# Counting the guard flag in pieces and reordering the last images of a ViT tower kernel

## The chip, the cores and the metric

The kernel runs on one core of one Trainium2 chip. The metric is the device time of one execution in microseconds (us); lower is better. The number of a kernel is the median of several runs.

## The reference

The reference is a small vision transformer tower on 32 images of 3x256x256 in float32. Every image gives 256 tokens of 256 features.

```python
h = tokenizer(x)                                   # 16x16 patches, a matmul
h = h + L0_attn(layernorm(h))                      # gated attention with squared relu
h = h + L0_ffn(layernorm(h))                       # top half of the tokens through an MLP
h = h + L1_attn(layernorm(h))                      # phase memory
h = h + L1_ffn(layernorm(h))                       # this change lies here
```

Only the last line matters for this change. The layer-1 FFN makes four heads of 64 features, gives each head four experts that are causal softmax attentions, mixes them by a gate, adds a residual, normalizes, runs two small layers with a norm, and weights the heads by a last gate:

```python
sx = einsum(x, hl_w) + hl_b                        # heads
qkv = softmax(causal(q k)) v                       # four experts of each head
qkv = where(sx == 0, 0, qkv)                       # pad
mixed = sum over experts of out * softmax(gate)
resid = sx[arange(nh), arange(nh)]                 # head n of image n: four images feed every image
hn = layernorm(mixed + resid)
hx = relu(where(fx == 0, 0, fx @ fc1.T + b1)); hx = where(fx == 0, 0, hx @ fc2.T + b2)
fout = layernorm(hx + fx)
out = fout * softmax(fout @ fgate_w.T)
```

The two `== 0` masks and the ranges of some intermediate values are not applied in the fast path. The kernel counts zeros and values out of range, and if any was found it runs a slow general version afterwards.

## The kernel before

The tower is one function, `vit_tower`, with the stages one after the other. The layer-1 FFN is the last stage. It works image by image. The work of an image is cut into 93 pieces (`PIECES`, numbered from 0), each a small function of the image `b`: `heads` (3), `heads_out` (4), `experts` (5 and 7), `scores` (12 to 17), `exponentials` (18 to 23), `later_keys` (24 to 29), `outputs` (31 to 38), the gates, `scaled` (65), `turn_e` (66), the two small layers (69 to 73), `head_gate` (78 to 86) and `last_norm` (87 to 91).

The order of all instructions is written out by hand. `tc.manual_schedule` keeps every engine in the order in which the program issues. `ROUND` is a list of pairs (back, piece): in round `r` the piece is issued for image `r - back`, so several images are in flight at different depths. When the heads of the last image (piece 3 of image 31) have been issued, `END` takes over: a list of (images from the end, piece) for the rest, so (0, k) is image 31, (1, k) is image 30, and so on.

What each engine does in this stage: TensorE (PE) runs the heads, scores, outputs and layers into eight PSUM banks (`bank()`); ScalarE (ACT) copies and exponentiates them; GpSimd (POOL) masks the later keys (`later_keys`, L1237); VectorE (DVE) does gates, norms and sums; SyncE (SP) issues the transfers, in order. Each engine works through its own queue in order.

Names that the change and the prediction touch:

- `residual` (piece 1, L1145 to L1151) multiplies four heads of images 0 to 3 by the identity into a bank ("bank<-ident,sx") and copies them to `res` on DVE; for image 3 it then runs `centred`, three DVE instructions (L667 to L669). It reads `im.sx`, which `heads_out` of the same image has just written on ACT (L1162).
- `res` is read by `summed` (piece 61, L1332) of every image.
- `count_zeros` (L1170) runs one DVE pass over a 128x512 tile and leaves a count in a column of `zeros` (64 columns: `sx` and `fxT` of each image).
- `check_ranges` (L1263) compares the `ranges` of eight images (128x384) with two limits and multiplies the results into `good`. It runs for images 7, 15 and 23 inside the stage and for 31 behind it.
- Behind the hand-written order come the sums (L1571 to L1583): `n_bad` is the number of bad ranges and zeros of each partition, a matmul with `ones` sums it over the partitions, and DVE copies the sum to `flag` as an integer.
- `again = nc.values_load(flag[0:1, 0:1])` (L1586) loads the flag on all five engines, and `tc.If(again > 0)` (L1587) jumps over `general`, the slow version, which has several hundred instructions.
- `last_norm` (L1458) makes the output of an image in the tile `fout`. That tile has one buffer, so the next image's first write waits until the output transfer of the image before it (`out_dram<-fout`, L1473) has read it.
- `eblk` is a tile of the same shape, into which `turn_e` writes for all images but the last. Image 31 is turned on PE instead.

Of the kernel before, what the change touches and what calls it, by code (L numbers as in the profile page):

```python
# [33 lines left out]
F32 = mybir.dt.float32  # L34
# [6 lines left out]
P = 128  # L41
# [39 lines left out]
def vit_tower(tc, a, out):  # L81
# [1027 lines left out]
    with (  # L1109
# [10 lines left out]
        def whole(im, name, shape, pool=None, key=None):  # L1120

            key = key or name
            if key not in im.whole:
                im.whole[key] = (pool or p1).tile(shape, F32, name=name)
            return im.whole[key]
# [42 lines left out]
                nc.sync.dma_start(im.sw[halves[1 - h], :, :], im.sx[halves[h], :, :])  # L1168

        def count_zeros(x, k):  # L1170
            junk = p1.tile([P, 2 * N], F32, name="junk")
            nc.vector.tensor_scalar(  # L1172
                junk, x.rearrange("p h n -> p (h n)"), 0.0, 0.0, ALU.is_equal, ALU.add, accum_out=zeros[:, k : k + 1]
            )
# [84 lines left out]
        def in_range(b, first, n):  # L1259
            return ranges[:, b // 8 % 2, b % 8, first : first + n]  # L1260

        def check_ranges(b):
            r = ranges[:, b // 8 % 2, :, :].rearrange("p b x -> p (b x)")  # L1263
            nc.vector.scalar_tensor_tensor(good, r, 1.0 / LOW, good, ALU.is_le, ALU.mult)
            nc.vector.scalar_tensor_tensor(good, r, 1.0 / HIGH, good, ALU.is_ge, ALU.mult)

        def small(name, shape):
            return spool.tile(shape, F32, name=name, tag=f"{name}_{shape[1]}", bufs=4)
# [187 lines left out]
                nc.vector.tensor_tensor(im.gate, im.gate, over(im.m, [P, NC, NH], 2), ALU.mult)  # L1456

        def last_norm(b, im, i):  # L1458
            f = whole(im, "fout", G8)
            if i == 0:  # L1460
                nc.vector.tensor_tensor(f, im.whole["ey"][:, :, 0:HD], over(im.rs, G8, 2), ALU.mult)  # L1461
            if i == 1:
                nc.vector.tensor_tensor(f, f, over(row_e("fn_g"), G8, 1), ALU.mult)
            if i == 2:
                nc.vector.tensor_tensor(f, f, over(row_e("fn_b"), G8, 1), ALU.add)  # L1465
            if i in (3, 4):
                for n in range(NH):
                    g, d = (i - 3) * NH + n, slice(n * HD, (n + 1) * HD)
                    nc.vector.scalar_tensor_tensor(  # L1469
                        f[:, g, :], f[:, g, :], im.gate[:, i - 3, n : n + 1], H[b][:, i - 3, d], ALU.mult, ALU.add  # L1470
                    )
            if i == 5:
                nc.sync.dma_start(  # L1473
                    out[b].rearrange("(c p) d -> p c d", p=P),
                    f.rearrange("p (c n) d -> p c (n d)", n=NH),
                )
# [17 lines left out]
            (squares_sum, 1), (root, 1), (head_gate, 0), (head_gate, 1), (head_gate, 2), (head_gate, 3),  # L1494
            (head_gate, 4), (head_gate, 5), (head_gate, 6), (head_gate, 7), (head_gate, 8), (last_norm, 4),
            (last_norm, 0), (last_norm, 1), (last_norm, 2), (last_norm, 3), (last_norm, 5),
            (features_moved,),
        )
        ROUND = (
            (-1, 84), (-4, 43), (-5, 27), (-4, 46), (-6, 5), (-5, 13), (-4, 44), (-6, 6), (-1, 85), (-1, 86),  # L1500
            (-1, 90), (-5, 19), (-5, 25), (-5, 12), (-5, 28), (-2, 2), (-2, 67), (-4, 47), (-4, 48),
            (-5, 14), (-5, 18), (-5, 24), (-1, 91), (-3, 60), (-4, 49), (-3, 61), (-5, 30), (-6, 7), (-6, 9),
            (-2, 69), (-4, 50), (-3, 62), (-7, 3), (-2, 92), (-5, 20), (-2, 68), (-4, 51), (-4, 52),
            (-3, 63), (-5, 26), (-5, 17), (-2, 70), (-6, 8), (-3, 64), (-7, 4), (-7, 1), (-6, 10), (-4, 53),
            (-6, 16), (-6, 11), (-6, 15), (-4, 54), (-2, 71), (-4, 55), (-5, 23), (-6, 22), (-5, 29),
            (-5, 34), (-4, 56), (-4, 57), (-5, 32), (-3, 65), (-5, 37), (-4, 58), (-3, 66), (-2, 72),
            (-2, 73), (-6, 21), (-2, 74), (-5, 42), (-4, 59), (-2, 75), (-2, 76), (-5, 45), (-9, 0),
            (-5, 33), (-2, 77), (-5, 31), (-2, 87), (-2, 78), (-2, 79), (-2, 89), (-5, 41), (-5, 39),
            (-5, 40), (-5, 38), (-2, 80), (-5, 35), (-2, 81), (-2, 88), (-2, 82), (-5, 36), (-2, 83),
        )  # L1510
        END = (
            (5, 68), (3, 51), (0, 2), (3, 52), (3, 53), (3, 55), (3, 54), (2, 20), (2, 17), (3, 56), (5, 92),
            (1, 10), (1, 11), (4, 63), (5, 70), (3, 57), (1, 8), (1, 16), (1, 15), (4, 64), (4, 65), (0, 4),
            (2, 26), (3, 58), (2, 23), (5, 71), (4, 66), (3, 59), (5, 73), (5, 72), (3, 60), (2, 29),
            (1, 21), (2, 32), (1, 22), (2, 31), (5, 74), (5, 75), (1, 30), (4, 2), (2, 36), (5, 76), (2, 37),
            (2, 45), (2, 38), (3, 61), (5, 77), (3, 62), (2, 39), (5, 87), (2, 34), (3, 63), (2, 40),
            (2, 33), (5, 78), (5, 89), (5, 79), (2, 46), (2, 35), (1, 14), (2, 44), (3, 64), (2, 43),
            (2, 42), (1, 13), (2, 41), (5, 88), (3, 65), (4, 67), (0, 5), (2, 47), (5, 80), (2, 48), (2, 49),
            (5, 81), (2, 50), (1, 20), (5, 82), (2, 51), (2, 52), (3, 66), (1, 19), (4, 92), (4, 69), (0, 6),
            (2, 53), (5, 83), (1, 12), (0, 7), (4, 70), (5, 84), (1, 27), (2, 54), (0, 9), (5, 85), (2, 55),  # L1520
            (2, 56), (1, 17), (2, 57), (5, 90), (5, 86), (1, 28), (1, 26), (0, 10), (2, 58), (1, 18),
            (1, 24), (0, 11), (0, 8), (2, 59), (0, 15), (1, 23), (1, 25), (0, 16), (4, 71), (3, 2), (4, 72),
            (1, 29), (1, 31), (0, 21), (0, 22), (5, 91), (4, 73), (4, 68), (2, 60), (1, 36), (0, 27),
            (1, 34), (1, 33), (4, 74), (3, 67), (4, 75), (1, 32), (1, 44), (2, 61), (4, 76), (2, 62),
            (1, 38), (1, 41), (1, 39), (4, 77), (4, 87), (1, 42), (4, 78), (4, 79), (2, 63), (1, 40),
            (4, 80), (4, 89), (2, 64), (1, 37), (2, 65), (1, 35), (2, 66), (4, 81), (1, 46), (1, 45),
            (0, 13), (0, 28), (1, 43), (4, 82), (1, 47), (1, 48), (0, 14), (0, 19), (1, 49), (4, 88),
            (3, 69), (0, 20), (1, 50), (4, 83), (0, 25), (3, 92), (1, 51), (1, 52), (3, 70), (0, 12),
            (1, 53), (3, 68), (0, 18), (4, 84), (0, 26), (4, 85), (1, 54), (2, 2), (1, 55), (0, 17), (4, 86),
            (0, 34), (0, 35), (0, 24), (0, 43), (1, 56), (0, 23), (0, 33), (0, 31), (0, 29), (1, 57),  # L1530
            (4, 90), (3, 71), (0, 39), (0, 41), (0, 42), (0, 32), (2, 67), (0, 36), (1, 58), (3, 72),
            (3, 73), (3, 74), (0, 38), (4, 91), (2, 92), (1, 59), (0, 44), (3, 75), (0, 40), (3, 76),
            (0, 37), (0, 46), (2, 69), (0, 45), (1, 60), (3, 77), (1, 61), (3, 78), (0, 47), (3, 79),
            (0, 48), (1, 62), (2, 70), (1, 63), (0, 49), (1, 64), (3, 87), (3, 80), (2, 71), (1, 65),
            (3, 81), (0, 50), (1, 66), (3, 82), (3, 83), (3, 89), (3, 84), (0, 51), (0, 52), (3, 88),
            (0, 53), (3, 85), (2, 68), (1, 2), (0, 54), (0, 55), (3, 86), (2, 72), (0, 56), (3, 90), (2, 73),
            (2, 74), (0, 57), (2, 75), (2, 76), (0, 58), (3, 91), (2, 77), (1, 67), (1, 69), (1, 92),
            (0, 59), (2, 78), (2, 87), (2, 79), (0, 60), (2, 80), (2, 89), (1, 70), (2, 81), (1, 71),
            (2, 82), (0, 61), (2, 83), (2, 88), (2, 84), (0, 62), (2, 85), (0, 63), (0, 64), (2, 90),
            (2, 86), (0, 65), (1, 72), (1, 73), (1, 74), (1, 68), (0, 66), (0, 67), (1, 75), (2, 91),  # L1540
            (0, 69), (0, 92), (1, 76), (1, 77), (0, 70), (1, 87), (0, 71), (1, 78), (1, 79), (1, 89),
            (1, 80), (1, 81), (1, 82), (1, 88), (1, 83), (1, 84), (0, 72), (1, 85), (0, 73), (1, 90),
            (1, 86), (0, 74), (0, 75), (0, 76), (0, 30), (0, 77), (1, 91), (0, 78), (0, 79), (0, 80),
            (0, 81), (0, 87), (0, 82), (0, 83), (0, 89), (0, 84), (0, 88), (0, 85), (0, 90), (0, 86),
            (0, 91), (0, 1), (0, 68),
        )
        LAST = PIECES.index((heads,))

# [10 lines left out]
        with tc.manual_schedule(engines={ENG.PE, ENG.DVE, ENG.Activation, ENG.Pool, ENG.SP}):  # L1559
# [3 lines left out]
            for b, k in order_e():  # L1563
                do, *i = PIECES[k]
                do(b, images[b], *i)
                if do == heads_out and b in LATE:
                    last_features(LATE[b])
        check_ranges(B - 1)


        n_bad = p1.tile([P, 2], F32, name="n_bad")  # L1571
        nc.vector.tensor_reduce(n_bad[:, 0:1], good, AX.X, ALU.add)
        nc.vector.tensor_reduce(n_bad[:, 1:2], zeros, AX.X, ALU.add)
        nc.vector.scalar_tensor_tensor(
            n_bad[:, 0:1], n_bad[:, 0:1], -1.0, n_bad[:, 1:2], ALU.mult, ALU.add
        )
        nc.vector.tensor_scalar(n_bad[:, 0:1], n_bad[:, 0:1], float(8 * N_RANGE), None, ALU.add)
        ones = p1.tile([P, 1], F32, name="ones")
        nc.vector.memset(ones, 1.0)
        p = bank()  # L1580
        mm(p[0:1, 0:1], n_bad[:, 0:1], ones)
        flag = cpool.tile([1, 1], mybir.dt.int32, name="flag")
        nc.vector.tensor_copy(flag, p[0:1, 0:1])  # L1583

    right_e.close()
    again = nc.values_load(flag[0:1, 0:1])  # L1586
# [385 lines left out]
```

## Time and profile before

| what | us |
|---|---|
| time, median of 3 runs | 1864.86 (1863.34 to 1864.94) |
| the profiled execution, its own time | 1866.7 |
| its span, from the first to the last instruction | 1864.9 |
| PE busy | 1815.6 (97%) |
| DVE busy | 1349.6 (72%) |
| ACT busy | 811.0 (43%) |
| POOL busy | 615.6 (33%) |
| mean granted TensorE clock | 0.987 of full speed |

Busy is the time in which an engine had an instruction in execution. The span is cut into 40 slices on the profile's page, each about 46.6 us, with the busy share of each engine in tenths. The layer-1 FFN begins at about 1243 us, in slice 27; the last image's heads (where `END` begins) run at 1778 us; the last arithmetic instruction starts at 1858.99 us.

### The profile page before, as it was taken

What the parts mean: (1) busy time and instruction counts of PE and PEld (TensorE: products, weight loads), DVE (VectorE), ACT (ScalarE), POOL (GpSimd) and SP (SyncE); (2) the same over time, 40 slices, a digit from 0 to 9 for tenths busy, and PEclk for the clock granted to TensorE, in tenths of its full rate; (3) what the DMA queues carried; (4) which work ended last, traced back from release to release, by engine and by line L of the source; (5) the groups of instructions that cost most, each with busy time, mean ns of one, the idle gap of its engine ahead of it and who ended that gap; (6) DMA issues with size and microseconds to landing.
All of it is one profiled execution on the core that took longest, in us unless ns stands there. A gap on an engine that the chain in (4) does not pass through costs nothing.

```text
span 1864.9 us, 36574 instructions
## 1 busy us (share of the span) xinstructions
PE 1815.6 (97%) x14282; PEld 1274.4 (68%) x14282; DVE 1349.6 (72%) x3592; ACT 811.0 (43%) x1640; POOL 615.6 (33%) x696
## 2 busy tenths in 40 slices
PE   9999999999999999999999999999999999999993
PEld 7887567676766677666654555567777887878871
DVE  2335377878787664543578887754899999999998
ACT  0001222222222211211345545547888888888882
POOL 1223143434343334332444334332223222232230
PEclk9999999999999999999999999999999999999995
DMA  9540222221212135333222222222344443443332
GB/s 302 159 152 27 46 45 58 54 60 48 55 45 58 43 106 152 96 116 93 88 77 80 79 79 80 79 68 54 95 106 107 105 108 101 105 108 103 102 94 59
DMA packets 193171, 167.50 MB, mean 90 GB/s; under 512 B 70880, under 2 KB 166112, under 8 KB 192608
## 3 DMA queue, kind: packets, MB, share of 16 engines
q1 hardware_dynamic: 186272, 147.51, 27.8%
q0 software_dynamic: 6144, 16.79, 3.0%
q8 instruction: 115, 1.88, 0.4%
q10 hardware_dynamic: 576, 0.79, 0.1%
q14 instruction: 64, 0.52, 0.1%
HBM read 82.98 MB, written 57.41 MB: 75 GB/s over the span
## 4 chain that ended last, share of the span: by engine, by line
PE 91%; DVE 6%; ACT 1%; DMA 1%; issue 1%; SPq 0%; ACTq 0%; DVEq 0%
PE bank L118 90%; DVE fout L1469 1%; DVE eo L1318 0%; DMA patch<-in_patches_dram 0%; PE bank L516 0%; DVE two L1326 0%; DVE ranges L1341 0%; DVE six L126 0%; DVE junk L1172 0%; DVE ey L1426 0%; ACT dex L945 0%; DVE dz L991 0%; DVE fout L1465 0%; DVE fout L1461 0%; DVE dxB L199 0%
## 5 line engine op out<-in xcount | busy, mean ns | idle before, releaser
L1237 POOL TENSOR_SCALAR_AFFINE_SELECT et<-et 128x512 f32<-128x512 f32 (+1 forms) x192 | 169.3, 891 | 397.0 <-ACT et L1228 282.2
L1228 ACT ACTIVATE et<-bank 128x512 f32<-128x512 f32 x384 | 203.1, 625 | 0.4 <-PE bank L118 0.3
L118 PE MATMUL bank<-ev,et 128*64 128x68 f32 (+1 forms) x6144 | 193.4, 224 | 0.8 <-POOL et L1237 0.6
L118 PEld LDWEIGHTS bank<-ev,et 128*64 128x64 f32 x6144 | 189.8, 137 | 3.8 <-issue 1.2
L118 PE MATMUL bank<-g,sw 64*128 64x256 f32 (+1 forms) x512 | 180.3, 490 | 0.0
L118 PE MATMUL bank<-g,sx 64*128 64x256 f32 (+1 forms) x512 | 179.3, 490 | 0.3 <-ACT g L1190 0.3
L118 PE MATMUL bank<-tokW,patch 128*128 128x256 f32 x768 | 166.8, 380 | 2.9 <-DMA patch<-in_patches_dram 2.9
L118 PEld LDWEIGHTS bank<-tokW,patch 128*128 128x128 f32 x768 | 146.1, 191 | 24.0 <-issue 3.8
L118 PE MATMUL bank<-bxT,w_wuv 128*128 128x512 f32 x300 | 134.5, 604 | 2.7 <-DMA bxT<-b_turned 2.7
L118 PEld LDWEIGHTS bank<-g,sx 64*128 64x128 f32 x512 | 92.2, 187 | 54.3 <-issue 45.0
L864 ACT ACTIVATE hT<-bank,cols 128x512 f32<-128x512 f32 x64 | 44.0, 687 | 186.9 <-PE bank L118 186.9
L118 PE MATMUL bank<-wvo,dm 128*128 128x512 f32 x256 | 114.3, 599 | 0.0
L118 PE MATMUL bank<-w_wo,gT 128*128 128x256 f32 x512 | 113.2, 379 | 0.0
L118 PE MATMUL bank<-attn,bv 128*128 128x256 f32 x512 | 113.1, 379 | 0.0
L118 PE MATMUL bank<-w_w,hT 128*128 128x256 f32 x512 | 112.3, 379 | 0.0
L118 PE MATMUL bank<-xsel,w_w 128*128 128x512 f32 x256 | 111.4, 592 | 0.0
L118 PEld LDWEIGHTS bank<-attn,bv 128*128 128x128 f32 x512 | 97.2, 190 | 19.6 <-issue 7.2
L126 DVE BATCH_NORM_STATS2 six<-h 128x6 f32<-128x256 f32 x256 | 105.5, 412 | 4.4
L118 PEld LDWEIGHTS bank<-w_w,hT 128*128 128x128 f32 x512 | 97.0, 190 | 15.6 <-issue 2.9
L118 PEld LDWEIGHTS bank<-w_wo,gT 128*128 128x128 f32 x512 | 97.2, 190 | 13.4 <-DVE gT L489 0.2
L118 PEld LDWEIGHTS bank<-bxT,w_wuv 128*128 128x128 f32 x300 | 58.0, 194 | 69.9 <-issue 68.9
L118 PE MATMUL bank<-w_wuv,bxT 128*128 128x512 f32 x240 | 105.4, 592 | 0.0
(286 smaller groups left out, 3570.3 us busy)
## 6 DMA issues: line engine op xcount, KB each, us to landing
patch<-in_patches_dram SPq DMA_DIRECT2D x31, 768.0 KB, 4.6
exT<-normed SPq DMA_DIRECT2D x32, 256.0 KB, 3.7
sw<-sx SPq DMA_DIRECT2D x64, 128.0 KB, 2.4
out_dram<-fout SPq DMA_DIRECT2D x32, 256.0 KB, 2.1
er_turned<-eblk SPq DMA_DIRECT2D x31, 256.0 KB, 2.7
fraw<-er_turned SPq DMA_DIRECT2D x62, 128.0 KB, 3.2
both<-fxT SPq DMA_DIRECT2D x62, 128.0 KB, 2.3
both<-hx SPq DMA_DIRECT2D x62, 128.0 KB, 2.3
```

The costliest lines, as they stand in the source:

```text
L118: nc.tensor.matmul(o, lhsT, rhs, start=first, stop=last)
L126: nc.vector.bn_stats(six, x)
L864: nc.scalar.activation(s.hT[:, m, :], p, AF.Gelu_apprx_tanh, bias=col("b1", m))
L1228: nc.scalar.activation(t2[:, i, :], p, AF.Exp)
L1237: nc.gpsimd.affine_select(out=own, in_=own, pattern=[[0, 2 * n_e], [1, P]], compare_op=ALU.is_ge, fill=0.0, base=0, channel_multiplier=-1,)
L1469: nc.vector.scalar_tensor_tensor(f[:, g, :], f[:, g, :], im.gate[:, i - 3, n : n + 1], H[b][:, i - 3, d], ALU.mult, ALU.add)
```

## The change

Four things, all in the layer-1 FFN.

1. **The flag.** Four new pieces (`count_bad`, 93 to 96) do the counting of image 31 inside the hand-written order: the ranges of images 24 to 30 first (336 wide), then the zeros, then the ranges of image 31 alone (48 wide), then the sum over the partitions and the copy to `flag`. In `END` all four stand ahead of the last image's `last_norm`. Two products instead of one add up in the bank.
2. **An output tile of its own.** `last_norm` of image 31 writes into `eblk` instead of `fout`.
3. **The residual's product later.** In `ROUND`, (-7, 1) became (-6, 1): the product of image b is issued one round later and no longer behind `heads_out` of the same image.
4. **A new `END`.** The list is ordered anew as a whole; it holds the same pieces and the four new ones. The `ones` column is set on POOL instead of DVE.

```diff
         def count_zeros(x, k):
+            done.add(k)
...
-        def check_ranges(b):
-            r = ranges[:, b // 8 % 2, :, :].rearrange("p b x -> p (b x)")
-            nc.vector.scalar_tensor_tensor(good, r, 1.0 / LOW, good, ALU.is_le, ALU.mult)
-            nc.vector.scalar_tensor_tensor(good, r, 1.0 / HIGH, good, ALU.is_ge, ALU.mult)
+        flag = cpool.tile([1, 1], mybir.dt.int32, name="flag")
+
+        def check_ranges(b, first=0, n=8, ok=None):
+            w = slice(first * N_RANGE, (first + n) * N_RANGE)
+            r = ranges[:, b // 8 % 2, first : first + n, :].rearrange("p b x -> p (b x)")
+            nc.vector.scalar_tensor_tensor(good[:, w], r, 1.0 / LOW, good[:, w], ALU.is_le, ALU.mult)
+            nc.vector.scalar_tensor_tensor(
+                good[:, w], r, 1.0 / HIGH, good[:, w], ALU.is_ge, ALU.mult, accum_out=ok
+            )
+
+        n_bad = p1.tile([P, 3], F32, name="n_bad")
+        ones = p1.tile([P, 1], F32, name="ones")
+        nc.gpsimd.memset(ones, 1.0)
+        done, count = set(), Image()
+
+        def count_bad(b, im, i):
+            if b < B - 1:
+                return
+            if i == 0:
+                check_ranges(B - 1, 0, 7)
+                nc.vector.tensor_reduce(n_bad[:, 0:1], good[:, 0 : 7 * N_RANGE], AX.X, ALU.add)
+            if i == 1:
+                count.zeros = min((k for k in range(2 * B) if k not in done), default=2 * B)
+                nc.vector.tensor_reduce(n_bad[:, 1:2], zeros[:, 0 : count.zeros], AX.X, ALU.add)
+                nc.vector.scalar_tensor_tensor(
+                    n_bad[:, 0:1], n_bad[:, 0:1], -1.0, n_bad[:, 1:2], ALU.mult, ALU.add
+                )
+                nc.vector.tensor_scalar(n_bad[:, 0:1], n_bad[:, 0:1], float(8 * N_RANGE), None, ALU.add)
+            if i == 2:
+                check_ranges(B - 1, 7, 1, n_bad[:, 2:3])
+                nc.vector.tensor_scalar(n_bad[:, 2:3], n_bad[:, 2:3], -1.0, None, ALU.mult)
+                p = count.p = bank()
+                parts = [n_bad[:, 0:1], n_bad[:, 2:3]] + [zeros[:, k : k + 1] for k in range(count.zeros, 2 * B)]
+                for k, x in enumerate(parts):
+                    mm(p[0:1, 0:1], x, ones, k == 0, k == len(parts) - 1)
+            if i == 3:
+                assert len(done) == 2 * B
+                nc.vector.tensor_copy(flag, count.p[0:1, 0:1])
...
         def last_norm(b, im, i):
-            f = whole(im, "fout", G8)
+            f = whole(im, "eblk" if b == B - 1 else "fout", G8)
...
-            (features_moved,),
+            (features_moved,), (count_bad, 0), (count_bad, 1), (count_bad, 2), (count_bad, 3),
         )
         ROUND = (
-            (-1, 84), (-4, 43), (-5, 27), (-4, 46), (-6, 5), (-5, 13), (-4, 44), (-6, 6), (-1, 85), (-1, 86),
+            (-1, 84), (-4, 43), (-5, 27), (-4, 46), (-6, 1), (-6, 5), (-5, 13), (-4, 44), (-6, 6), (-1, 85),
...
-            (-3, 63), (-5, 26), (-5, 17), (-2, 70), (-6, 8), (-3, 64), (-7, 4), (-7, 1), (-6, 10), (-4, 53),
+            (-4, 52), (-3, 63), (-5, 26), (-5, 17), (-2, 70), (-6, 8), (-3, 64), (-7, 4), (-6, 10), (-4, 53),
...
+            (-1, 93), (-1, 94), (-1, 95), (-1, 96),
         )
         END = (
...
-            (0, 81), (0, 87), (0, 82), (0, 83), (0, 89), (0, 84), (0, 88), (0, 85), (0, 90), (0, 86),
-            (0, 91), (0, 1), (0, 68),
+            (1, 75), (0, 68), (0, 71), (2, 86), (0, 93), (2, 91), (0, 72), (0, 73), (1, 76), (0, 74),
+            (1, 77), (0, 94), (0, 75), (1, 78), (0, 76), (0, 95), (1, 79), (0, 77), (1, 87), (1, 80),
+            (0, 78), (0, 96), (1, 81), (0, 79), (1, 82), (0, 87), (0, 80), (1, 89), (0, 81), (0, 82),
+            (1, 83), (0, 89), (1, 84), (0, 83), (1, 88), (1, 85), (0, 88), (0, 84), (1, 90), (0, 85),
+            (1, 86), (0, 90), (0, 86), (1, 91), (0, 91), (0, 1),
         )
...
-        check_ranges(B - 1)
-
-
-        n_bad = p1.tile([P, 2], F32, name="n_bad")
-        nc.vector.tensor_reduce(n_bad[:, 0:1], good, AX.X, ALU.add)
-        nc.vector.tensor_reduce(n_bad[:, 1:2], zeros, AX.X, ALU.add)
-        nc.vector.scalar_tensor_tensor(
-            n_bad[:, 0:1], n_bad[:, 0:1], -1.0, n_bad[:, 1:2], ALU.mult, ALU.add
-        )
-        nc.vector.tensor_scalar(n_bad[:, 0:1], n_bad[:, 0:1], float(8 * N_RANGE), None, ALU.add)
-        ones = p1.tile([P, 1], F32, name="ones")
-        nc.vector.memset(ones, 1.0)
-        p = bank()
-        mm(p[0:1, 0:1], n_bad[:, 0:1], ones)
-        flag = cpool.tile([1, 1], mybir.dt.int32, name="flag")
-        nc.vector.tensor_copy(flag, p[0:1, 0:1])
```

## The prediction, made before the changed kernel ran

> **What bounds the kernel now.** I read the busy slices first, then a table of stretches for the end, the timeline behind it, the branch's instructions, and last the waits on the residual.
>
> The 40 slices of 46.6 us:
>
> ```profile
> PE   9999999999999999999999999999999999999993
> ...
> DVE  2335377878787664543578887754899999999998
> ```
>
> PE is full to the last slice, DVE only from slice 28 on. In 20 us stretches between 1600 and 1760 PE is busy all 20.00 us and DVE some 14: there PE is the bound. Behind the last image's heads (1778) it is DVE. The stretches of the end (busy time of PE, PEld, DVE, ACT, POOL, then PE clock, DMA share, GB/s):
>
> ```profile
> 1779.00:1790.00 11.00, 11.00 (x249) 9.21 (x249) 11.00 (x19) 8.17 (x22) 4.04 (x4) 1.00 0.38 98
> 1810.00:1820.00 10.00, 9.44 (x238) 8.00 (x234) 9.61 (x26) 7.26 (x17) 3.58 (x4) 1.00 0.58 151
> ...
> 1840.00:1850.00 10.00, 6.26 (x52) 3.75 (x49) 8.52 (x29) 3.96 (x8) 0.00 (x0) 0.50 0.08 28
> 1850.00:1859.14 9.14, 0.19 (x2) 0.11 (x2) 8.56 (x33) 0.72 (x3) 0.00 (x0) 0.50 0.17 58
> sum 80.14, PE 52.84 PEld 39.13 DVE 77.31 ACT 44.53 POOL 14.07; mean PE 6.61 PEld 4.89 DVE 9.66 ACT 5.57 POOL 1.76
> ```
>
> DVE works 77.31 of the 80.14 us, so all that a new END can win from waits is 2.83 us. The timeline of DVE and PE there:
>
> ```profile
> 1847.33 0.44 DVE L1426 TENSOR_TENSOR ey<-bank,c_row 128x272 f32<-128x272 f32 x1 [0.56 <-PE bank L118]
> 1848.24 0.44 DVE L1426 TENSOR_TENSOR ey<-bank,c_row 128x272 f32<-128x272 f32 x1 [0.39 <-PE bank L118]
> ...
> 1857.30 0.68 DVE L1172 TENSOR_SCALAR_CACHE_REDUCE junk<-fxT 128x512 f32<-128x512 f32 x1
> ...
> 1858.77 0.19 PE L118 MATMUL bank<-ones,n_bad 128*1 128x1 f32 x2 [10.57 <-DVE n_bad L1577]
> 1858.99 0.15 DVE L1583 CAST flag<-bank 1x1 int32<-1x1 f32 x1 [0.37 <-PE bank L118]
> ```
>
> Of the 2.83 us, .95 are the two waits of image 31 for PE, .37 the flag's, .48 two waits for ACT's gates; the rest are small gaps. Behind the flag the load and the branch:
>
> ```profile
> L1586 DVEq TENSOR_LOAD <-flag x1: 543/543/543, 1859.2 to 1859.2; - x1
> ...
> L1587 PEldq COMPARE_BRANCH  x1: 4044/4044/4044, 1859.8 to 1859.8; - x1
> ...
> L1587 DVEq EVENT_SEMAPHORE  x1: 21/21/21, 1863.2 to 1863.2; - x1
> L1587 PEldq EVENT_SEMAPHORE  x1: 51/51/51, 1863.9 to 1863.9; - x1
> ```
>
> ACT and SP go on .45 us after their branches, DVE only at 1863.2 and PE at 1863.9; the span ends 1.07 later. So 5.8 us pass behind the flag, and PE is the last to come back.
>
> **The residual (image 0 to 3).** Four products wait for ACT's `sx`: .62, .56, 1.01 and .96 us. Two of them:
>
> ```profile
> 1263.37 0.54 PE L118 MATMUL bank<-ident,sx 64*128 64x64 f32 x3 [1.01 <-ACT sx L1162]
> ...
> 1282.23 0.32 PE L118 MATMUL bank<-ident,sx 64*128 64x64 f32 x1 [0.96 <-ACT sx L1162]
> ```
>
> PE is the bound there, so a wait that goes is time won. A round later `sx` is long written; the product itself (.45 us) moves and is no cost. Image 0 keeps its place in the order of PE: 0. Image 1: its exponentials leave ACT at 1253.89 and PE would wait for them at 1253.95 anyway: 0 (bounds 0 to -.56). Image 2: PE runs 1 us ahead, but the next outputs need POOL's mask, which ends at 1267.40: -.7 (0 to -1.0). Image 3: -1.0 (0 to -1.0). Sum **-1.7**, bounds 0 to -2.6. Past what it moves: scores and outputs in PE's queue; four `res` copies (.25 each) and once `centred` (.69+.42+.69) in DVE's, in rounds where DVE has 5.8 of 20 us free. Without that cover the last would cost 1.8 once. No transfer moves with it, and SP and POOL are not passed. The `ones` column (59 ns on DVE) goes to POOL, busy 33%: nothing; without that cover it would cost its 59 ns.
>
> **END: waits and added work.** From the end of image 31's norm (1840.57) I set out the new DVE order with the durations of before. DVE has 6.6 us of work until the first `ey` of image 31, which PE delivers at +6.8 and +7.7; waits of about .6 stay, since PE's small layers at clock 0.5 form the same chain. What follows (counts, gate, image 30's and 31's norms) ends at +18.3. The gates keep .3 of waiting and small gaps .5, so 1.4 of the 2.83 stay: -1.4. The copy to `flag` waits for PE's product (.37 before); queued behind it are 18 DVE instructions of the last norms, and the list puts about .5 us of other DVE work ahead of it, so it should not wait; if that cover is gone, +.4. Image 31's own tile takes away its wait for image 30's output transfer. Image 30's first `fout` write needs image 29's transfer landed at +7.4 and comes at +10.3.
>
> Added: the ranges twice more, narrow. A 64-wide operation of this kind issues every .20 us, a 384-wide takes .55, so 1.04 ns per column: two 48-wide .40, accumulator read .08, one scalar .16, minus the 48 columns saved three times, .15: **+.5**. [...] The trace has 64-wide ones .20 apart, so I stay with .5. Together -1.4 + .5 = **-.9**: DVE's last instruction ends at 1858.2.
>
> **The branch.** With the flag about 7 us earlier, PE, ACT and POOL load and branch beneath the norms; PE's 4.0 us disappear. DVE still comes behind its own norms: its load and return took 4.05 from the flag's end, PE's 4.74, so the end follows .7 sooner: at least -.65. If DVE's sequencer runs ahead of its engine, the load starts before the last operation ends: by one operation (.28) about -.9. The trace does not show it. [...] then SP's last transfer sets the end (issue .37, landing 2.1 to 2.2, load .48 and resets: last operation + 4.1), in all -1.65. I take **-.85**, nearest to the row (the load followed the flag's end by .03), with ends -.65 and -1.65. On the other side: the out transfer of image 31 is now issued at DVE's very end, hidden beneath DVE's 4.05; without that cover the end is 4.1 behind, still 1.7 sooner than 5.8.
>
> **POOL against DVE.** While POOL still masks (1779 to 1820), the same operations are slower than in the rounds; the groups of 1779 to 1820, then those of 1600 to 1779:
>
> ```profile
> L1469 DVE SCALAR_TENSOR_TENSOR fout<-fout,fgate,h 128x64 f32<-128x64 f32 x16 | 5.4, 400 | 0.0
> L1326 DVE TENSOR_TENSOR two<-eo 128x1024 f32<-128x1024 f32 x3 | 4.8, 1600 | 0.0
> ```
> ```profile
> L1469 DVE SCALAR_TENSOR_TENSOR fout<-fout,fgate,h 128x64 f32<-128x64 f32 x80 | 16.6, 280 | 0.4
> L1326 DVE TENSOR_TENSOR two<-eo 128x1024 f32<-128x1024 f32 x10 | 12.2, 1216 | 0.0
> ```
>
> About 4.3 us of DVE time over some 13 masks, .33 each, against .14 in the rounds. A new order deals out anew which operations meet a mask. Ends: at the rounds' rate -2.3, at double the excess +4.3; I take **-.5**, since the mix of operations hardly changes.
>
> **Sum.** -1.7 - .9 - .85 - .5 = -3.95. The profiled execution took 1866.7 (span 1864.9 and 1.8 around it), 1.84 over the median; both move by the same. 1866.7 - 3.95 = 1862.75, in the median 1864.86 - 3.95 = **1860.9**.
>
> **The rivals.**
>
> 1. *More is won* (0.33). END's collisions fall to the rounds' rate (-2.3 in place of -.5), and DVE's queue runs ahead (-1.65 in place of -.85): 1858.3. For it: DVE in END meets masks more than twice as dearly as elsewhere. Against: the same masks and operations are there.
> 2. *A wait takes the place of the old* (0.22). In SP's order image 30's `hx` loads stand behind image 28's output, which waits for DVE's last norm of 28. I estimate .6 to 3 us until DVE reaches image 30's `ey`; if it comes 1 us late, and image 2 wins nothing, the sum loses 1.7: 1862.6.
> 3. *The change does not do what it says* (0.04). The residual's waits only change their releaser (the mask, a bank), and the engines leave the branch together: only -.9 and -.5 remain, 1863.5.
> 4. *Slower* (0.05). The masks of images 29 to 31 on POOL, 1779 to 1816, fall on DVE's two-input operations. One mask costs .33 now. The worst single 64-wide one took 1.1 us where .28 is usual, so .83 can be lost. From +.30 per mask over 13 masks (3.9 us) the sum is eaten; at +.6 it is 1868.7, slower than before. Against it: the average over 13 masks would have to reach the worst.
>
> My own case has 0.36, within 1859.4 to 1862.4.
>
> **The numbers.** 0.2% of the time, 3.7 us, is about what a measurement of this kernel can tell from no change, so faster begins below 1861.1. My case lies on that edge: .25 of its .36 count as faster, as the unknown sizes of branch and collisions lean down. Faster .33 + .25 = 0.58, same .11 + .22 + .04 = 0.37, slower 0.05. The range 1857.4 to 1864.0 leaves out case 4, half of case 3 and the tails of 1 and 2.
>
> **What would show it.** Right: no wait for ACT's `sx` at the products of images 2 and 3, and the stages behind them 1.7 us ahead; PE's branch before the last `fout`; DVE's idle time between heads and end down from 2.8 to about 1.4; the last DVE operation a 64-wide one of image 31; DVE's semaphore 4 us behind it, and the end less than 5 behind it. Wrong: an idle row of DVE over 1 us with SP or a transfer named as releaser, the mean of the 64-wide row above 400 ns, the mean of the 1024-wide above 1600, or PE as late as before at 1779.

## The result, and the profile after

The changed kernel takes 1856.10 us (median of 6 runs, 1854.23 to 1860.63) where the kernel before takes 1864.16 (6 runs, 1863.05 to 1865.87): 8.06 us less. The ratio is 0.9958 with a 95% interval of 0.9949 to 0.9968. Beside the experiments the same kernel took 1855.88 us (5 runs), ratio 0.9950 (0.9937 to 0.9964). The forecast was 1860.9, range 1857.4 to 1864.0: the direction was right, but the time lies below the range, and the gain is twice the 3.95 us that were forecast.

The execution in the profile after is the slowest of its six (own time 1860.63, span 1858.9). It entered the layer-1 FFN .7 us later than that of before (image 0's heads leave ACT at 1245.58, before 1244.84), and between 1330 and 1603 us TensorE lost 1.2 us (before: .2) in short gaps with no releaser. The profiles of this case enter the stage at times that lie up to 5.8 us apart: ahead of it the granted TensorE clock falls to 0.5 for 3.4 us at a time, 6.8 us in all in the profile before, none in the second profile of the changed kernel. So below I compare stretches between the same instructions, not whole spans.

(One correction to the numbers of pieces above: `head_gate` is 77 to 85, and `last_norm` is 86 to 91, 86 being its last four sums.)

The busy slices of the page after:

```profile
PE   9999999999999999999999999999999999999993
...
DVE  2335477878888664543578778764899999999998
```

The picture is as before: TensorE until the last image's heads, then VectorE. The stretches of the end (same columns as before), from the same heads to DVE's last operation:

```profile
1779.06:1790.00 10.94, 10.94 (x249) 9.14 (x249) 10.58 (x23) 9.03 (x24) 2.76 (x4) 1.00 0.39 99
...
1830.00:1854.91 24.91, 9.53 (x76) 5.34 (x74) 24.00 (x87) 6.54 (x16) 0.00 (x0) 0.50 0.20 53
sum 75.85, PE 51.75 PEld 38.52 DVE 74.33 ACT 43.63 POOL 14.77; mean PE 8.63 PEld 6.42 DVE 12.39 ACT 7.27 POOL 2.46
```

DVE is idle for 75.85 - 74.33 = 1.52 us, before 2.83. But the stretch shrank by 4.3 us, so busy time went too. The timeline of the end:

```profile
1844.54 0.44 DVE L1461 TENSOR_TENSOR ey<-bank,c_row 128x272 f32<-128x272 f32 x1 [0.47 <-PE bank L118]
...
1847.92 0.14 DVE L1300 CAST flag<-bank 1x1 int32<-1x1 f32 x1
...
1852.49 0.86 DVE L1504 SCALAR_TENSOR_TENSOR fout<-fout,fgate,h 128x64 f32<-128x64 f32 x4
1853.27 1.64 DVE L1504 SCALAR_TENSOR_TENSOR eblk<-eblk,fgate,h 128x64 f32<-128x64 f32 x8
1854.94 0.37 SPq L1508 DMA_DIRECT2D out_dram<-eblk  x1
```

One of the two waits for `ey` is left, the flag's copy waits for nothing, and DVE's last operation is a 64-wide one of image 31, as forecast. The load and the branch:

```profile
L1606 DVEq TENSOR_LOAD <-flag x1: 544/544/544, 1852.6 to 1852.6; - x1
...
L1607 PEldq COMPARE_BRANCH  x1: 3669/3669/3669, 1848.7 to 1848.7; - x1
...
L1607 PEldq EVENT_SEMAPHORE  x1: 51/51/51, 1852.4 to 1852.4; - x1
L1607 DVEq COMPARE_BRANCH  x1: 76/76/76, 1853.2 to 1853.2; - x1
...
L1607 DVEq EVENT_SEMAPHORE  x1: 21/21/21, 1856.1 to 1856.1; - x1
```

TensorE branches beneath the norms and is back 2.5 us before DVE ends. DVE's load starts 2.3 us before DVE's last operation ends (1854.91). The end comes 4.0 behind that operation; before it was 5.8 behind the flag's copy. The residual's products of images 2 and 3 no longer wait:

```profile
1272.59 0.54 PE L118 MATMUL bank<-ident,sx 64*128 64x64 f32 x3
...
1289.08 0.32 PE L118 MATMUL bank<-ident,sx 64*128 64x64 f32 x1
```

And the two groups from 1779 to 1820:

```profile
L1361 DVE TENSOR_TENSOR two<-eo 128x1024 f32<-128x1024 f32 x3 | 4.9, 1643 | 0.0
L1504 DVE SCALAR_TENSOR_TENSOR fout<-fout,fgate,h 128x64 f32<-128x64 f32 x12 | 2.5, 272 | 0.0
```

The 1024-wide sums are as slow as before (1600); their mean of 1643 is one of the signs that the prediction named for being wrong, though a small one, .13 us over three. The 64-wide ones went from 400 ns to 272, what they take with no mask beside them (276 and 273 in the two runs without masks).

The 8 us in three parts, each between two instructions that both kernels have:

| part | before | after | change |
|---|---|---|---|
| image 0's heads to image 4's on ACT (residual) | 54.23 | 52.43 | -1.80 |
| last gate of `ROUND` on DVE (1776.8) to DVE's last operation | 82.37 | 78.03 | -4.34 |
| from there to the end of the span | 5.80 | 4.01 | -1.79 |

The sum is -7.9. The second profile of the changed kernel has 78.03 and 4.01 again, so its DVE stretch repeats. The output tile of its own was in no run alone. In the new order image 31's first write to it (1848.14) comes ahead of image 30's output transfer (1853.37), so what it does is to make that order possible.

### The profile page after: what moved, and what is told of

Its sections match the earlier page's. It is cut to its first block, busy times and chain, and to the rows that moved or that the text cites. A ratio compares the mean times of both kernels' runs of the same rounds, so it can differ in the third digit from the quotient of the medians.

```text
span 1858.9 us, 36581 instructions
## 1 busy us (share of the span) xinstructions
PE 1814.4 (98%) x14284; PEld 1277.1 (69%) x14284; DVE 1345.4 (72%) x3595; ACT 810.0 (44%) x1640; POOL 614.0 (33%) x697
## 4 chain that ended last, share of the span: by engine, by line
PE 92%; DVE 5%; ACT 1%; DMA 1%; issue 1%; SPq 0%; DVEq 0%; ACTq 0%
PE bank L118 91%; DMA patch<-in_patches_dram 0%; PE bank L516 0%; DVE eo L1353 0%; DVE fout L1504 0%; DVE ranges L1376 0%; DVE six L126 0%; ACT dex L945 0%; DVE two L1361 0%; ACT et L1229 0%; ACT two L945 0%; DVE dz L991 0%; DVE dxB L199 0%; DVE dx L837 0%; DMA b_turned<-blocks 0%
## 5 line engine op out<-in xcount | busy, mean ns | idle before, releaser
L118 PE MATMUL bank<-ev,et 128*64 128x72 f32 (+1 forms) x6144 | 194.0, 225 | 2.5 <-ACT et L1229 1.3
```

What stands on the lines that cost most here:

```text
L118: nc.tensor.matmul(o, lhsT, rhs, start=first, stop=last)
```

## The experiments

The table gives DVE's stretch and the tail as in the last two rows above, and the ratio of the times to those of the kernel before.

| kernel | DVE stretch | tail | median us | ratio (95%) |
|---|---|---|---|---|
| before | 82.37 | 5.80 | 1864.2 | 1 |
| changed, again | 78.03 | 4.01 | 1855.9 | 0.9950 (0.9937 to 0.9964) |
| residual alone | 82.40 | 5.84 | 1862.4 | 0.9990 (0.9984 to 0.9997) |
| flag alone | 81.53 | 5.23 | 1862.7 | 0.9992 (0.9985 to 0.9998) |
| flag alone, as filling | 81.10 | 6.1 | 1863.1 | 0.9994 (0.9985 to 1.0002) |
| changed, flag last | 81.15 | 5.91 | 1860.6 | 0.9981 (0.9974 to 0.9988) |
| changed, flag's copy later | 78.08 | 4.88 | 1858.7 | 0.9966 (0.9954 to 0.9978) |
| before, no masks | 79.69 | 6.0 | 1862.0 (1 run) | - |
| changed, no masks | 76.08 | 4.0 | 1855.8 (1 run) | - |
| changed, tail in series | 79.04 | 4.0 | 1857.8 | 0.9965 (0.9951 to 0.9979) |
| changed, wide gate | 75.40 | 5.1 | 1854.5 | 0.9948 (0.9935 to 0.9962) |
| changed, wide gate for five | 75.31 | 4.01 | 1853.7 | 0.9948 (0.9934 to 0.9961) |
| the same, output in halves | 75.65 | 4.36 | 1854.2 | 0.9949 (0.9935 to 0.9962) |

### The changed kernel again

> The changed kernel itself, for a second profile and more times beside the kernel before. Theory A (three gains that add up, as the first two profiles say: residual -1.8, the new END -4.3 on DVE from 1776.8 on, branch -1.7): -7.8 us against before, ratio about 0.9958, and the second profile shows the same three sums. Theory B (the first profile's END was a lucky deal of collisions between DVE and POOL): END's share differs by over 1 us between the two profiles, and the ratio's interval is wide.

Measured -8.3 us. The stretch, the tail and the operations held up by masks are the same as in the first profile, to .02 us. Theory A holds, B falls.

### The residual alone

```diff
-            ..., (-7, 4), (-7, 1), (-6, 10), ...
+            ..., (-4, 46), (-6, 1), (-6, 5), ...
```

> The kernel before with the residual's product one round later, nothing else. Theory A: -1.8 us (ratio 0.9990): images 2 and 3 lose their waits of 1.01 and .96 and the stage behind runs 1.8 ahead to the last image's heads; END and the branch as before. Rival: the lead is lost again at the entry of END, since DVE is the bound there and was at work without a gap: then DVE's last instruction comes less than 1 us earlier and the ratio is within 0.0005 of 1.

Measured -1.8 us (-3.0 to -.6 by the interval). TensorE's timeline (idle before, with its releaser, in the brackets):

```profile
1251.74 0.91 PE L118 MATMUL bank<-sx,A 64*128 64x256 f32 x5 [0.91 <-ACT et L1228]
1263.61 4.66 PE L118 MATMUL bank<-ev,et 128*64 128x72 f32 x144 [1.31 <-ACT et L1228]
...
1270.11 0.54 PE L118 MATMUL bank<-ident,sx 64*128 64x64 f32 x3
```

Image 1's wait of .56 comes back as .91 for ACT's exponentials, and at image 2 TensorE now waits 1.31 for the same. Eight kernels with the new residual (the changed one, flag last, flag's copy later, without masks, tail in series and the three with a wide gate) show the same steps against before, to .02 us: 0 up to image 2's heads, -.56 at image 3's, -1.80 at image 4's. In the residual alone and the second profile of the changed kernel the steps fall short by .47 and .77: a gap of TensorE without a releaser (.24 and .53) lies in between, and TensorE's busy time there is .21 longer. The lead is not lost at the entry of `END`, where stretch and tail are those of before: the rival falls.

### The flag alone

```diff
+            (0, 77), (0, 68), (0, 93), (0, 94), (0, 95), (1, 91), (0, 78), (0, 79), (0, 96), (0, 80),
-            (0, 77), (1, 91), (0, 78), (0, 79), (0, 80),
...
-            (0, 91), (0, 1), (0, 68),
+            (0, 91), (0, 1),
```

> The kernel before with the counting in pieces ahead of image 31's last norm, and the flag's copy five DVE operations behind the product; old END, old residual, image 31 still writes to fout. Theory A (the branch is hidden by VectorE's queue and TensorE's early branch): the end follows DVE's last operation by 4.0 instead of 5.8, and the flag's wait of .37 is gone: -2.1 plus .2 of added work, about -1.9 us (ratio 0.9990), plus up to .95 if the counts fill the two waits for ey. Rival (my first value): the sequencer runs ahead by one operation only: -.9 to -1.2.

Measured -1.5 us. DVE's stretch fell by .8, but that is not the flag's doing: 1.0 was won ahead of the first operation that was moved, where a 1024-wide sum (.7) and a gate's product (.4) met no mask this time. From the start of the last `ey` to its end the stretch takes 11.10 where it took 10.90 with the flag's wait of .37 in it, so the added operations cost .57. The tail fell by .6 only, not by 1.8, though DVE was back at 1857.7, 1.9 us behind its last operation. What was late was the last output:

```profile
L1508 SPq DMA_DIRECT2D out_dram<-fout x1: 372/372/372, 1855.9 to 1855.9; - x1
...
DMA to landing us min/median/max: 3.4/3.4/3.4
```

In the changed kernel the last output lands in 2.14 us. In the trace's records of transfers a 16 KB packet of the instruction queue runs from 1856.40 to 1857.70, while the output's 272 packets run. Neither theory had this.

### The flag alone, as filling

```diff
+            (1, 84), (0, 68), (0, 30), (0, 93), (0, 94), (0, 72), (1, 85), (0, 73), ...
-            (1, 84), (0, 72), (1, 85), (0, 73), ...
```

> flag_only with the two zero counts and the ranges of images 24 to 30 put ahead of image 31's first ey, where DVE waited .55 and .39 us; old END, old residual, fout. Theory A (counting is worth most as filling for those waits): DVE's stretch falls from 81.5 to 80.6, and the end follows it by 4.0 to 5.2. Rival (what waits there comes later as well, since PE's small layers of image 31 hang on DVE work that is now behind the counts): 81.5 as before.

The two waits for `ey` are gone, but the stretch fell by .43, not .9: a wait of .61 for ACT behind them is new. The landing was slow again (transfer issued at 1857.12, SP's last semaphore 4.4 us behind it, in the changed kernel 2.3; packet of the instruction queue from 1858.20 to 1859.85), the tail 6.1, and no gain can be told in the time. In the old order the counts fill half a wait.

### The changed kernel with the flag last

```diff
-            ... (0, 93), ... (0, 94), ... (0, 95), ... (0, 96), ...
+            (1, 86), (0, 90), (0, 86), (1, 91), (0, 91), (0, 1), (0, 93), (0, 94), (0, 95), (0, 96),
```

> The changed kernel with its four counting pieces moved behind the last norm, as in the kernel before; new END, own tile and new residual stay. Theory A: the branch's 1.7 and the flag's wait of .4 come back, and the counts no longer fill waits: +2.0 to +2.8 against the changed kernel, -5.3 us against before (ratio 0.9972). Rival (END's gain comes from the counts filling the waits for ey): +3.5 or more against the changed kernel.

Against the changed kernel +4.7 us in the medians, +5.0 in stretch and tail: the rival. DVE now waits where the counts were:

```profile
1837.34 0.44 DVE L1461 TENSOR_TENSOR ey<-bank,c_row 128x272 f32<-128x272 f32 x1 [1.59 <-PE bank L118]
1838.24 0.44 DVE L1461 TENSOR_TENSOR ey<-bank,c_row 128x272 f32<-128x272 f32 x1 [0.47 <-PE bank L118]
1839.38 0.69 DVE L1376 TENSOR_REDUCE ranges<-esq 128x8 f32<-128x512 f32 x1 [0.60 <-ACT esq L1372]
1840.68 0.19 DVE L1469 TENSOR_TENSOR lg<-ey,fv 128x32 f32<-128x32 f32 x1 [0.29 <-ACT fv L1384]
```

These are 2.95 us of waits; the changed kernel has .47 of them. DVE's stretch is 3.1 us longer, and 2.8 of that are waits over .1 us. So the new `END` without the flag in it takes only 1.2 us off DVE's stretch, the flag in the old `END` by itself (without the masks that it happened to miss) adds .2, and both together take off 4.3. The counts are work that depends on nothing in flight, and the new order uses them to cover TensorE's small layers at clock 0.5.

### Masks left out

```diff
         def later_keys(b, im, k):
+            if b >= B - 3:
+                return
```

> The kernel before without GpSimd's masks of images 29 to 31 (their later keys stay unmasked; those are all masks that fall into END). Theory A (a GpSimd mask holds up the VectorE operation that meets it; 2.8 us of such hold-ups in the profile of before, .7 in the changed kernel): from the last gate of the rounds to the flag DVE takes 82.4 - 2.8 = 79.6 us, and all 48 narrow operations of L1469 take .28. Theory B (they are long for another reason, such as their place behind a wide operation or the transfers): the stretch stays within .7 of 82.4.

> The changed kernel with the same masks left out. Theory A: its DVE stretch has only .7 to 1.9 us of hold-ups left (two at the 1024-wide sum, one small one), so 78.0 becomes 76.1 to 77.3, and the gap between the two kernels shrinks from 4.3 to 2.0 - 2.9 us. Theory B (collisions are not what tells the two apart): the gap stays at 4.3.

The groups of `before_nomask` from 1776 to 1818, and DVE's waits in its stretch (total, times, longest):

```profile
L1328 DVE TENSOR_TENSOR two<-eo 128x1024 f32<-128x1024 f32 x3 | 3.6, 1201 | 0.0
L1471 DVE SCALAR_TENSOR_TENSOR fout<-fout,fgate,h 128x64 f32<-128x64 f32 x16 | 3.4, 276 | 0.0
```
```profile
DVE sm_m L1310 <- ACT gate L1307: 1.0, 2, 0.7
DVE ey L1428 <- PE bank L118: 0.9, 2, 0.6
DVE ranges L1343 <- ACT esq L1339: 0.6, 1, 0.6
```

Every operation falls to its usual length, 400 to 276 ns and 1600 to 1201: the masks on POOL made them long, theory A. A hold-up is the time by which an operation takes longer than the same operation of the run without masks. Counted so, from .06 us up, there are 4.45 us of hold-ups in the kernel before and 2.19 in the changed one, more than the 2.8 and .7 that I had started from. The stretch of before fell by 2.7 us to 79.69. That this is the figure expected is luck: more hold-ups went, and new waits took part of their place. The changed kernel fell by 1.95, so the gap is 3.6 without masks, not 2.0 to 2.9: expectation missed. In the old order 1 us of new waits came up where the hold-ups had been (1.0 for ACT's gate instead of .6, .6 for `esq`). In the changed order nothing came up:

```profile
DVE ey L1463 <- PE bank L118: 0.5, 1, 0.5
DVE sm_m L1345 <- ACT gate L1342: 0.3, 1, 0.3
DVE ranges L1378 <- ACT esq L1374: 0.3, 1, 0.3
```

So of the 4.34 us, .7 is what masks cost the old order more than the new. The other 3.6 are there without any mask.

### The tail in series

```diff
+            (1, 81), (0, 96), (1, 82), (1, 89), (1, 83), (1, 84), (1, 88), (1, 85), (1, 90), (1, 86), (1, 91),
+            (0, 78), (0, 79), (0, 80), (0, 81), (0, 87), (0, 82), (0, 83), (0, 89), (0, 84), (0, 88), (0, 85),
+            (0, 90), (0, 86), (0, 91), (0, 1),
```

> The changed kernel with the gates and norms of images 30 and 31 one behind the other, as in the kernel before, not interleaved; flag, own tile and all else stay. Theory A (interleaving two chains covers the latency between dependent small operations): DVE's last stretch, from the last ey to the end, grows from 10.1 to about 10.8 us, waits for ACT's two exponentials of .2 to .3 each come on top, together +.6 to +1.2 us. Rival (the interleaving itself is worth nothing, END won only by collisions and by filling the waits for ey): within .2.

Theory A: the stretch is 1.01 longer, all of it behind the start of the last `ey` (11.37 for 10.37), with no wait over .1. Image 31's gate in the kernel before, then in this run:

```profile
1853.01 0.16 DVE L1442 TENSOR_TENSOR fgate<-fgate,fg_row 128x8 f32<-128x8 f32 x1
1853.20 0.16 DVE L1445 TENSOR_REDUCE sm_f<-fgate 128x2 f32<-128x8 f32 x1
1853.39 0.17 DVE L1447 TENSOR_TENSOR fgate<-fgate,sm_f 128x8 f32<-128x8 f32 x1
```
```profile
1848.62 0.17 DVE L1477 TENSOR_TENSOR fgate<-fgate,fg_row 128x8 f32<-128x8 f32 x1
1848.82 0.16 DVE L1480 TENSOR_REDUCE sm_f<-fgate 128x2 f32<-128x8 f32 x1
1849.02 0.17 DVE L1482 TENSOR_TENSOR fgate<-fgate,sm_f 128x8 f32<-128x8 f32 x1
```

Each depends on the one before and starts .19 to .20 behind it. In the changed kernel the small operation of one image stands between those of the other, and two such start .07 to .08 apart:

```profile
1847.99 0.15 DVE L1482 TENSOR_TENSOR fgate<-fgate,sm_f 128x8 f32<-128x8 f32 x1
1848.07 0.15 DVE L1477 TENSOR_TENSOR fgate<-fgate,fg_row 128x8 f32<-128x8 f32 x1
1848.14 0.68 DVE L1496 TENSOR_TENSOR eblk<-ey,fv 128x512 f32<-128x512 f32 x1
```

The medians differ by 1.9 us, more than stretch and tail, with intervals that overlap.

### The flag's copy later

```diff
-            (0, 78), (0, 96), (1, 81), ...
+            (1, 83), (0, 89), (1, 84), (0, 96), (0, 83), ...
```

> The changed kernel with only the flag's copy later, by about 2.2 us (behind image 30's reciprocal); the counts stay. TensorE then branches 2.2 us later, at about T-4.0 instead of T-6.2 before DVE's end T, and is still back before the end. Theory A (the lead of the flag counts because TensorE's second 16 KB packet of code, 4.3 us behind its branch, must not meet the last output transfer): that packet falls from T+.3 on, the transfer's landing grows from 2.15 to 3.0 - 3.5 us as in flag_only, and the end follows T by 4.9 to 5.3 instead of 4.0: +1 us against the changed kernel; DVE's stretch stays 78.0. Rival (any lead of the flag that covers TensorE's return is enough; flag_only's slow landing was chance): 4.0 again, within .2.

Theory A, at its low end: DVE's stretch is 78.08, TensorE is back at 1851.9, before DVE's end at 1852.47, and the tail is 4.88. The output transfers:

```profile
L1508 SPq DMA_DIRECT2D out_dram<-fout x1: 378/378/378, 1850.9 to 1850.9; - x1
L1508 SPq DMA_DIRECT2D out_dram<-eblk x1: 373/373/373, 1852.5 to 1852.5; - x1
...
DMA to landing us min/median/max: 2.7/2.9/3.0
```

The instruction queue's second 16 KB packet ran from 1852.63 to 1853.90, into the last output. In the changed kernel it ended at 1854.31, .6 before that transfer was issued; there it met image 30's output, which landed in 2.68 us. With the flag last, where no such packet runs until both outputs have landed, both take 2.14, though they follow each other just as closely. So the slow landings here, 2.68 to 3.0 us, came with the packet and not with the other output alone. The time is 2.9 us worse in the medians; .87 of it is in the tail and none in DVE's stretch; the intervals overlap.

### Wide gate

```diff
+                if b >= B - 6:    # in wide_gate5: if B - 6 <= b < B - 1
+                    # first call: f *= gate, second: f += h, each 128x512
```

> The changed kernel with the gate and the last sum of images 26 to 31 as two 512-wide operations instead of eight 64-wide ones. By the issue distances (8 x .196 = 1.57 against 2 x .60 = 1.20) .37 us less for each image. Theory A (DVE is the bound through all of END): -2.2 us against the changed kernel. Rival (the wait for image 31's ey absorbs what is saved before it): only images 30 and 31 count, -.7, and that wait grows from .5 to about 1.9. For the branch: DVE's load of the flag is issued behind the last operation that waits for a semaphore; here that is the last or last but one, so the load starts .6 to 1.3 before the end instead of 2.3, DVE comes back later than the transfer lands, and .3 to 1.0 of the gain is lost again.

The stretch fell by 2.6 and the tail rose by 1.1, as theory A has it in both. But 1.4 of the 2.6 are hold-ups that went, mostly since two 1024-wide sums met no mask in this run, and .7 came back as idle time. What is left is 1.9, or .3 an image, a little under the .37 of the working. The end of the tail:

```profile
1848.29 0.69 DVE L1507 TENSOR_TENSOR eblk<-eblk,h 128x512 f32<-128x512 f32 x1
```
```profile
L1613 DVEq TENSOR_LOAD <-flag x1: 826/826/826, 1848.3 to 1848.3; - x1
...
L1614 DVEq EVENT_SEMAPHORE  x1: 21/21/21, 1852.8 to 1852.8; - x1
```

The load starts with the last operation, the one that waits for the product, and DVE is back 3.8 us behind its end. But the last output is late here too: fifteen of its sixteen semaphore updates came by 1851.14, the last at 1852.29, 3.3 us behind the issue, and SP goes on only then. Without that DVE's return would have set the end, by my estimate from SP's waits about .3 us sooner. Why the landing was late is open: the 16 KB packet had ended at 1848.54, before the issue at 1849.01.

> Two 512-wide operations for the gate and the last sum of images 26 to 30, eight narrow ones for image 31. Theory A (the load of the flag starts with the last VectorE operation that waits for a semaphore, here the first of the eight narrow ones, 1.6 us before the end, and is back before the transfer lands): DVE's stretch is .4 longer than with all six wide (75.8), but the end follows it by 4.0 and not by 5.1: -2.2 us against the changed kernel, ratio to before about .9943. Rival (the tail of 5.1 has another cause than the late load, such as the shape of the last operation or a slow landing by chance): the tail stays above 4.6.

```profile
1845.22 1.65 DVE L1511 SCALAR_TENSOR_TENSOR eblk<-eblk,fgate,h 128x64 f32<-128x64 f32 x8
```
```profile
L1613 DVEq TENSOR_LOAD <-flag x1: 541/541/541, 1844.7 to 1844.7; - x1
...
L1614 DVEq EVENT_SEMAPHORE  x1: 21/21/21, 1848.2 to 1848.2; - x1
```

With image 31 left narrow the load is 2.2 us ahead of DVE's end (1846.87) and the tail 4.01 again. Since the output lands in 2.13 us here too, the run doesn't rule out that a slow landing by chance made part of the 5.1. At 1853.7 us this version is 2.2 us below the changed kernel in the medians (-2.7 in stretch and tail), the fastest of this case; its interval overlaps that of the changed kernel.

```diff
+            if b == B - 1 and i in (3, 5):
+                c = 0 if i == 3 else 1
+                nc.sync.dma_start(out[b][c * P : (c + 1) * P, :], ...)
```

> wide_gate5 with image 31's output sent in two transfers, the first half when its four narrow operations are done. Theory A (the landing of the last transfer sets the end, 2.15 us of which about .4 are the second half's data): -.2 to -.4 us against wide_gate5. Rival (the landing is latency, the size does not matter, or DVE's return comes just behind it): within .1.

No gain: the tail is 4.36, the time within the scatter. The second half was issued .32 us behind DVE's end, since SP was still issuing image 30's output, and landed 2.26 us behind its issue, where the whole output took 2.13. Half the size didn't land sooner: the rival.

## Why the prediction fell short, by its own steps

| step | forecast | measured |
|---|---|---|
| residual | -1.7 | -1.80 |
| `END`: waits | -1.4 | waits over .1 us: 2.21 to .98, -1.23 |
| added counting | +.5 | +.57 (flag alone) |
| POOL against DVE | -.5 | hold-ups 4.45 to 2.19, -2.26; -.7 net by the masks left out |
| spacing of operations | 0 | -1.4, what is left of the -4.34 |
| branch | -.85 | -1.79 |

**Residual.** Right in sum and place: -.56 from image 2's product (forecast -.7), -1.24 from image 3's (-1.0), nothing from images 0 and 1. That the sum is so close is in part luck, since image 3's share lies beyond the bound of -1.0 that I gave it, and image 2's is short; no run divides them further. The mask on POOL was named as what would catch image 2; it was ACT's `et`.

**END.** The failed step is the forward working of DVE's busy time in `END`: waits, counts and collisions together were put at -1.4 us, and the stretch fell by 4.34. The idle term in it was right (-1.4, measured -1.23), and the counts' cost too. The working gave DVE's last operation at 1858.2; counted from the same gate as before, it came at 1854.8.

Two terms were mis-sized. The first is the spacing. I had set out the new order "with the durations of before", so with the old spacing of the small operations, for chains that the new order interleaves; that put spacing at nothing, and what is left of the stretch is -1.4. The run in series shows 1.0 us of it for images 30 and 31 alone.

The second is the collisions. I had taken their mix as unchanged ("the mix of operations hardly changes"), and so -.5. The new order lets none of the 48 narrow operations meet a mask (before 4, for 1.97 us), so its hold-ups fall by 2.26, about the -2.3 that I gave as the one end. The working's 4.3 us for the old hold-ups was right in size (4.45). But the runs without masks say that much of this would have gone into other waits in the old order, and only .7 is net.

How the 3.6 us that are left without masks divide isn't a plain sum, since each part hides another: by the records of the two kernels without masks, waits over .1 fall from 3.26 to 1.07, and the rest is 1.4, or 2.0 with the added counts set against it. How much of that rest is spacing was measured for the tail only.

The working had the counts ahead of image 31's first `ey`, but charged them as added work of .5 and did not see that they carry the new order: without them there the waits are 2.95. This didn't spoil the number, since with the counts in place the idle term came right.

**Branch.** DVE's load did run ahead: it started 2.3 us before DVE's last operation ended (1852.62 to 1854.91), with eleven narrow operations ahead of it not yet started. The value taken was wrong: I put -.85 beside ends of -.65 and -1.65, by the row nearest at hand (a load .03 behind the flag). It was -1.79, the far end. That row could not tell, since the load there waited for the flag itself. (The 18 DVE instructions that I counted behind the flag's copy are 31 in the trace.) That the load would start as early as the far end needs, no row of before showed. That the output's landing then sets the end at +4.1 was worked out and held: 4.0.

**Narrow operations.** The narrow counts cost .57, near the .5 of the working. Small operations of DVE that depend on each other started .19 to .20 apart (tail in series), against .07 to .08 where the other image's stood between (changed kernel), and at the gate two 512-wide operations beat eight 64-wide ones by about .3 us an image (wide gate).

**Rivals.** Case 1 (more is won, 1858.3) had the direction, the size of the hold-ups and, for the branch, the cause; it too missed the spacing. No wait on SP for image 30's `hx` showed (case 2). Case 3 and case 4 fall.

## What to carry to other kernels

When an order is laid out anew, count the distance between starts and not only durations and waits: here a chain of small dependent operations cost .19 to .20 a step alone and .07 to .08 where another chain stood between. Keep work that depends on nothing, such as counting, for the place where the bound engine would wait for another (here .47 us of waits with the counts there, 2.95 without). For a branch at the end, ask when VectorE's last waiting instruction is released, since here its load of the flag started .04 to .06 us behind that, and let the flag be early enough that the instruction queue's packets don't meet the last output (a tail .87 us longer here).

## What the runs showed of the hardware that was not expected

- With the flag ready, DVE's load of it started .04 to .06 us behind the result for which the last waiting DVE operation waited, in the changed kernel with eleven operations not yet started, in the flag alone with seven, in the wide gate with none.
- Behind TensorE's taken branch two 16 KB packets ran in the instruction queue: in the profile before from 1860.74 and 1864.48 (branch at 1859.8), in the changed kernel from 1849.70 and 1853.03 (branch at 1848.7). The second came 4.0 to 4.7 us behind the branch in these two, the flag alone, the flag as filling and the flag's copy later. Where it met the last 256 KB output, that landed in 3.0 and 3.4 us instead of 2.14 (flag's copy later, flag alone); in the wide gate the last output landed 3.3 us behind its issue with no such packet beside it.
- Each of the four 64-wide DVE operations that met a mask on POOL in the kernel before ended .07 us behind the mask: they took .65 to .67 where masks of .6 to .7 ran, and 1.11 beside one of 1.18.
- DVE's stretch was 78.03 us in both profiles of the changed kernel, and the hold-ups by masks in it were the same to .02 us.
